# A list scheduler that keeps 64-column TensorE operations together, and attention weights made by a ScalarE Relu in the first three units

## The chip, the cores and the metric

The kernel runs on one core of a Trainium2 chip. The metric is device time in microseconds. The engines are named as the profile names them: PE is TensorE (PEld its weight loads), DVE is VectorE, ACT is ScalarE, POOL is GpSimd, SP is the queue that issues most transfers. Three timed runs of the kernel before are given, and one profiled execution.

## The reference

Input `x` has 64 graphs of 256 nodes with 256 features, and `adj` a 256 x 256 matrix of 0 and 1 for each graph. Four layers follow one another; each adds to `x` what it computes from `h = max(layernorm(x), 0)`.

- Layers 0 and 1 are graph attention with four heads of 64 columns. With `Wh = h W`, a score `e[i, j] = leaky_relu(src[i] + dst[j])` is masked by `adj`, goes through a softmax over `j`, and weighs `Wh`: `out[i] = sum_j softmax_j(e[i, j]) Wh[j]`. The slopes are 0.2 and 0.01. Layer 0 ends with an ELU; layer 1 adds a bias, a Relu, a residual and a layer norm over each head.
- Layer 2 is the same attention with one head of 256 columns (slope 0.2).
- Layer 3 is a gated graph network: three times, `m = h w[i]`, an aggregate over the neighbours `A^T m`, and a GRU cell with gates `r`, `z` and `n`.

## The kernel before, in words

The work is cut into 33 units: unit 0 is one graph, units 1 to 31 are two graphs each, unit 32 is the last graph. `graphs` (L976) describes a unit's four layers as operations. Nodes lie on the 128 partitions, so a unit of two graphs has four chunks of 128 nodes.

The softmax is taken apart. `factors` (L1077) makes, for each head, `cb`, the exponential of a node's score along a row, copied to all partitions, and `f`, two columns of exponentials for each partition. For the first two units `cb` comes from TensorE (`spread`, L1086); for the others it goes through DRAM (L1123, L1124). `weights` (L1139) builds the unnormalised weights `pt`: for each graph and half of its nodes a multiply by `f[1]` and a maximum with `f[0]` (L1145, VectorE, 256 columns), then for the whole head a minimum with `cap` (VectorE, 1024 columns). `cap` is made from the adjacency: it is huge where there is an edge and 0 or nearly 0 elsewhere, so the minimum is the mask. `attend_heads` (L1168) multiplies: for two heads, 32 matmuls whose weights are 128 x 64 pieces of `pt` and whose moving operand is `wh`, 65 columns, the last of which is 1 and gives the sum; two such matmuls with 64 columns each stand side by side in the array (L1163). `scaled` (L1180) then takes the reciprocal `rs` of the sum and writes `o`. Layer 2 uses the full 128 columns (L1163 too, 257 moving columns).

`gru` has, for each of three iterations and each half `j` of the features, four gates in PSUM banks from `ht` and `whh` and from the aggregate `ag` and `wc` (L1375, 512 moving columns; the bulk of TensorE's work). ScalarE applies tanh (L829, `g<-bank,bg` and `g<-g,bg`), VectorE combines them into the new `ht` half by half. Then each half of `ht` is transposed (L1389), split into two parts `hl` by a ScalarE copy and a VectorE subtraction, and aggregated (L1361); ScalarE copies the result to `ag`.

Every operation is recorded with an engine, a cost, what it reads and writes, and is put in order by `_Schedule.run` (L656). That is a list scheduler run when the program is built: it keeps a clock, a queue of operations that are ready for each engine, ordered by due time, and starts on an idle engine the first one whose buffers are free (L641). An operation is over after its cost, less an overlap of 90 on ScalarE and 80 on VectorE, and its result reaches another engine after a hop (OVERLAP and HOP, in ns). Operations marked `port` share one port between VectorE and POOL in this plan. What comes out is a fixed order of instructions on each engine, which the hardware then follows; the plan's times are not used again. So a changed cost can move operations far from the place where it was changed. Elementwise helpers record under one line, L829; the statistics are at L997 and L998, POOL's power at L1006, L1007, L1296 and L1297, the normalising Relu at L1015, `ht`'s first transposes at L1032, the projections at L1054, the masks at L1220 and L1230, the addition of layer 1 to `xt` at L1308.

Of the kernel before, what the change touches and what calls it, by code (L numbers as in the profile page):

```python
# [12 lines left out]
AF = mybir.ActivationFunctionType  # L13
# [503 lines left out]
SCORE_MAX = 40.0  # L517
SLOPES = (0.2, 0.01, 0.2)
SPREAD = 2
PACE = 104000.0  # L520


# [16 lines left out]
class _Op:  # L539
    __slots__ = (  # L540
        "engine", "cost", "port", "emit", "group", "bufs", "takes", "nbytes", "succs", "waits", "due", "ready",
        "index",
    )


class _Schedule:
# [28 lines left out]
    def buf(self, cls, shape, dtype=F32, tile=None):  # L575
        return _Buf(cls, shape, dtype, tile)

    def op(self, engine, cost, emit, reads=(), writes=(), takes=(), nbytes=0, port=False):
        o = _Op()
        o.port = port  # L580
        o.engine, o.cost, o.emit, o.group, o.nbytes = engine, cost, emit, self.group, nbytes
        o.succs, o.index, o.ready = [], len(self.ops), 0.0
        deps, o.bufs, o.takes = set(), [], []
        for written, items in ((False, reads), (True, writes)):
            for item in items:
                b, part = item if isinstance(item, tuple) else (item, None)
                if b not in o.bufs:
                    o.bufs.append(b)
                    b.left += 1
                if written and b.tile is None and b not in o.takes:  # L590
                    o.takes.append(b)
                keys = list(b.parts) if part is None else [k for k in (part, None) if k in b.parts]
                for k in keys:
                    writer, readers = b.parts[k]
                    if writer is not None:
                        deps.add(writer)
                    if written:
                        deps.update(readers)
                writer, readers = b.parts.get(part, (None, []))
                if written:  # L600
                    if part is None:
                        b.parts.clear()
                    b.parts[part] = (o.index, [])
                else:
                    b.parts[part] = (writer, readers + [o.index])
        for b in takes:
            if b.tile is None and b not in o.takes:
                o.takes.append(b)
        deps.discard(o.index)
        o.waits = len(deps)  # L610
        for d in deps:
            self.ops[d].succs.append(o)
        self.ops.append(o)
        return o
# [17 lines left out]
                )  # L632
            self.last[i.engine] = i.name

    def enable(self, ops, able):
        for o in ops:
            o.waits -= 1
            if o.waits == 0:
                heapq.heappush(able[o.engine], (o.due, o.index))

    def roomy(self, o):  # L641
        need = {}
# [13 lines left out]
    def run(self):  # L656
# [12 lines left out]
        events = []  # L669
        clock = self.dma_free = self.port_free = 0.0  # L670
        count = 0

        def post(t, kind, o):
            nonlocal count
# [8 lines left out]
        while True:  # L683
            for e in engines:
                if not idle[e]:
                    continue
                if e == "sp" and self.dma_free > clock + self.DMA_AHEAD:
                    continue
                held = []
                while able[e]:  # L690
                    item = heapq.heappop(able[e])
                    o = ops[item[1]]
                    if (not o.port or self.port_free <= clock) and self.roomy(o):
                        self.start(o, clock)
# [12 lines left out]
            while events and events[0][0] == clock:  # L707
                _, _, kind, o = heapq.heappop(events)
                if kind == "free":
                    idle[o.engine] = True  # L710
                    if o.nbytes:
                        self.dma_free = max(self.dma_free, clock) + o.nbytes / self.DMA_RATE
                        post(self.dma_free + self.DMA_LATENCY, "done", o)
                        post(max(clock, self.dma_free - self.DMA_AHEAD), "dma", o)
                    else:
                        post(clock + self.OVERLAP[o.engine] + self.HOP[o.engine], "done", o)
                    if o.engine == "pe":
                        self.enable([s for s in o.succs if s.engine == "pe"], able)
                elif kind == "done":
                    done += 1  # L720
                    self.enable([s for s in o.succs if s.engine != "pe" or o.engine != "pe"], able)
# [9 lines left out]
def _fast_path(  # L731
# [34 lines left out]
    nc = tc.nc  # L766
# [209 lines left out]
    def graphs(u, first, nb):  # L976
# [100 lines left out]
        def factors(wh, heads, width, slope, shift):  # L1077
# [55 lines left out]

            exps(0, 1.0)
            exps(1, slope)
            op("pool", 150, lambda: nc.gpsimd.memset(wh.tile[:, :, :, width], 1.0), [], [wh])  # L1136
            return f, cb

        def weights(cap, f, cb, h):  # L1139

            pt = buf("pt", [P, nb, 2, N])

            def emit(b, jc):
                c = 2 * b + jc
                nc.vector.tensor_scalar(  # L1145
                    pt.tile[:, b, jc, :].rearrange("p (i n) -> p i n", n=P),
                    cb.tile[:, h, 2 * b : 2 * b + 2, :],
                    f.tile[:, 1, h, c : c + 1], f.tile[:, 0, h, c : c + 1], op0=OP.mult, op1=OP.max,
                )

            for b in range(nb):
                for jc in range(2):
                    op("dve", 425, lambda b=b, jc=jc: emit(b, jc), [(cb, h), f], [(pt, (b, jc))], port=True)
# [14 lines left out]
        def attend_heads(o, o_view, pts, wh, hs):  # L1168
# [365 lines left out]
```

## Time and profile before

| what | value |
|---|---|
| median of three runs | 3197.43 us (3197.04 to 3197.9) |
| profiled execution, first to last instruction | 3198.1 us |
| mean granted TensorE clock in it | 0.996 |
| busy: PE, DVE, ACT, POOL | 3143.2, 2321.4, 1486.8, 897.4 us |
| matmuls of the gates, L1375, `wc` and `whh` | 1063.0 and 1055.6 us |
| matmuls with 64 weight columns, L1163, 128x65 | 263.7 us in 8192 records |
| multiply and maximum of the weights, L1145 | 416.9 us in 1152, 430 ns each |
| minimum with `cap`, 128x1024 | 326.1 us in 279, 1213 ns each |

The profile gives no time for its execution other than this span, which is 0.2 to 1.1 us longer than the timed runs. Matmuls of f32 leave two records each, transposes one. The duration of one instruction is longer than the distance between the starts of two neighbours, because they overlap; where many stand in a row the distance is what counts. A wait in brackets is idle time before the instruction, and what ended it.

### The profile page before, as it was taken

The page shows a single profiled execution, that of the slowest core. Times are in us where ns is not written, and L with a number is a line of the kernel's source. Part 1 is how long each engine was busy: PE and PEld are TensorE (multiplying, and loading weights), DVE is VectorE, ACT ScalarE, POOL GpSimd, SP SyncE. Part 2 cuts the span into 40 slices and gives each one's busy share as a digit, 9 for nine tenths or more (in the row PEclk, how much of TensorE's full clock was granted, in tenths as well). Part 3 has the DMA queues.
Part 4 walks back from the last instruction along what each step waited for, and adds up shares of the span by engine and source line. Part 5 has one row for each costly group of instructions (what it writes and reads, how often), then busy time and mean ns, then how long its engine had stood idle before and what let it go on. Part 6 is the DMA issues. An engine that isn't in the chain of part 4 may idle for free.

```text
span 3198.1 us, 48707 instructions
## 1 busy us (share of the span) xinstructions
PE 3143.2 (98%) x18599; PEld 1931.9 (60%) x18599; DVE 2321.4 (73%) x5206; ACT 1486.8 (46%) x3128; POOL 897.4 (28%) x907
## 2 busy tenths in 40 slices
PE   7899999999999999999999999999999999999998
PEld 6765656565666655566656566556566556665555
DVE  7777867778767778767678677788677787677753
ACT  5454444454454444454444454544444444544433
POOL 4323332133331233331233321333311333311210
PEclk9999999999999999999999999999999999999999
DMA  4110111101111101111101111111111011101000
GB/s 129 34 49 29 54 54 34 47 31 50 54 54 34 47 31 50 54 47 34 53 28 54 53 36 45 40 41 54 54 34 47 31 50 50 47 23 44 11 16 12
DMA packets 109927, 138.82 MB, mean 43 GB/s; under 512 B 44714, under 2 KB 97524, under 8 KB 102004
## 3 DMA queue, kind: packets, MB, share of 16 engines
q1 hardware_dynamic: 105712, 134.25, 12.8%
q8 instruction: 149, 2.44, 0.3%
q10 hardware_dynamic: 3972, 1.36, 0.2%
q14 instruction: 94, 0.77, 0.1%
HBM read 109.84 MB, written 17.34 MB: 40 GB/s over the span
## 4 chain that ended last, share of the span: by engine, by line
PE 87%; DVE 9%; POOL 2%; ACT 1%; issue 1%; DMA 0%; SPq 0%; ACTq 0%; POOLq 0%; DVEq 0%
PE bank L1375 55%; PE bank L1054 10%; PE bank L1163 10%; PE bank L1361 5%; PE bank L1032 3%; PE bank L1389 2%; DVE pt L1145 2%; DVE g L829 2%; DVE pt L829 1%; POOL mean L1297 1%; POOL o L829 1%; DVE o L829 1%; ACT ht L829 1%; DVE xt L1308 1%; DVE mean L829 1%
## 5 line engine op out<-in xcount | busy, mean ns | idle before, releaser
L1375 PE MATMUL bank<-ag,wc 128*128 128x512 f32 (+1 forms) x2376 | 1063.0, 582 | 0.0
L1375 PE MATMUL bank<-ht,whh 128*128 128x512 f32 (+1 forms) x2376 | 1055.6, 580 | 2.2 <-ACT g L829 1.3
L829 ACT ACTIVATE g<-bank,bg 128x512 f32<-128x512 f32 (+1 forms) x594 | 395.2, 670 | 713.6 <-PE bank L1375 706.6
L1375 PEld LDWEIGHTS bank<-ag,wc 128*128 128x128 f32 x2376 | 441.4, 190 | 459.2 <-issue 441.1
L1375 PEld LDWEIGHTS bank<-ht,whh 128*128 128x128 f32 x2376 | 435.0, 190 | 438.9 <-issue 424.2
L1006 POOL TENSOR_SCALAR mv<-mv 128x4 f32<-128x4 f32 (+1 forms) x132 | 81.9, 621 | 1428.6 <-DVE mv L998 1383.6
L1145 DVE TENSOR_SCALAR pt<-cb,f 128x256 f32<-128x256 f32 x1152 | 416.9, 430 | 6.0 <-ACT cb L1099 5.2
L1163 PEld LDWEIGHTS bank<-wh,pt 128*64 128x64 f32 (+1 forms) x8704 | 345.6, 142 | 94.4 <-issue 76.1
L829 DVE SCALAR_TENSOR_TENSOR g<-g,g 128x512 f32<-128x512 f32 (+1 forms) x396 | 263.3, 670 | 180.4 <-ACT g L829 180.4
L1163 PE MATMUL bank<-wh,pt 128*64 128x65 f32 (+1 forms) x8704 | 382.0, 233 | 9.7 <-DVE pt L829 5.8
L829 DVE TENSOR_TENSOR pt<-pt,cap 128x1024 f32<-128x1024 f32 (+1 forms) x297 | 341.3, 1193 | 0.1
L829 DVE SCALAR_TENSOR_TENSOR g<-bank,g 128x512 f32<-128x512 f32 (+1 forms) x198 | 129.8, 666 | 280.2 <-PE bank L1375 280.0
L829 DVE SCALAR_TENSOR_TENSOR g<-g,ht 128x512 f32<-128x512 f32 (+1 forms) x198 | 136.5, 689 | 172.0 <-ACT g L829 171.6
L1361 PE MATMUL bank<-am_r,hl 128*128 128x256 f32 x1536 | 238.1, 304 | 0.1
L1015 ACT ACTIVATE xn<-xt,mv 128x256 f32<-128x256 f32 x384 | 197.3, 588 | 72.1 <-DVE mv L829 71.9
L1361 PEld LDWEIGHTS bank<-am_r,hl 128*128 128x128 f32 x1536 | 198.2, 189 | 42.5 <-issue 30.6
L829 ACT COPY ag<-bank 128x512 f32<-128x512 f32 (+1 forms) x198 | 113.4, 573 | 233.4 <-PE bank L1361 230.1
L829 ACT ACTIVATE g<-g,bg 128x512 f32<-128x512 f32 (+1 forms) x198 | 137.6, 709 | 161.6 <-DVE g L829 159.4
L997 DVE BATCH_NORM_STATS2 st<-xt 128x6 f32<-128x256 f32 x512 | 208.1, 406 | 6.4 <-DMA xt<-in_x_dram 6.2
L829 ACT COPY ht<-bank 128x512 f32<-128x512 f32 (+1 forms) x264 | 137.8, 573 | 124.0 <-PE bank L1032 123.8
L1136 POOL MEMSET wh<- 128x16 f32 (+3 forms) x99 | 11.8, 120 | 635.5 <-ACT f L1130 635.5
L1007 POOL TENSOR_TENSOR mv<-mv,nhalf 128x4 f32<-128x4 f32 (+1 forms) x132 | 176.0, 1333 | 11.0
(91 smaller groups left out, 3452.2 us busy)
## 6 DMA issues: line engine op xcount, KB each, us to landing
cb<-rd SPq DMA_DIRECT2D x60, 1024.0 KB
xt<-in_x_dram SPq DMA_DIRECT2D x31, 512.0 KB
at<-in_adj_dram SPq DMA_DIRECT2D x31, 512.0 KB
out_dram<-xt SPq DMA_DIRECT2D x31, 512.0 KB
cb<-rd SPq DMA_DIRECT2D x30, 256.0 KB
cap<-cap_n SPq DMA_TRANSPOSE x128
cb<-rd SPq DMA_DIRECT2D x2, 512.0 KB
rd<-row ACTq DMA_DIRECT2D x60, 8.0 KB
```

Source lines behind the costliest of these rows:

```text
L829: emit = lambda: fn(*[a() if callable(a) else a for a in args], **kw)
L997: nc.vector.bn_stats(st.tile[:, c, :], xt.tile[:, c, :])
L1006: nc.gpsimd.tensor_scalar(mv.tile[:, 2, :], mv.tile[:, 1, :], 1e-5, None, op0=OP.add)
L1007: nc.gpsimd.tensor_tensor(mv.tile[:, 2, :], mv.tile[:, 2, :], nhalf[:, :C], op=OP.pow)
L1015: op("act", 610, lambda: nc.scalar.activation(xn.tile[:, c, :], xt.tile[:, c, :], AF.Relu, bias=mv.tile[:, 3, c : c + 1], scale=mv.tile[:, ...
L1032: nc.tensor.transpose(ps.tile[:, c * P : (c + 1) * P], xn.tile[:, c, dc * P : (dc + 1) * P], ident)
L1054: nc.tensor.matmul(ps.tile[:, : heads * W], lhsT=ht.tile[:, dc, c * P : (c + 1) * P], rhs=we[:, dc].rearrange("p h w -> p (h w)"), start=( ...
L1145: nc.vector.tensor_scalar(pt.tile[:, b, jc, :].rearrange("p (i n) -> p i n", n=P), cb.tile[:, h, 2 * b : 2 * b + 2, :], f.tile[:, 1, h, c ...
L1163: nc.tensor.matmul(ps[q * Q : (q + 1) * Q], lhsT=pt.tile[:, b, jc, i0 : i0 + Q], rhs=wh.tile[:, h, 2 * b + jc, :w], start=(jc == 0), stop= ...
L1361: nc.tensor.matmul(ps.tile[:, b * N : (b + 1) * N], lhsT=hl.tile[:, k, 2 * b + sc, :], rhs=am.tile[:, 2 * b + sc, :], start=(k == 0 and sc ...
L1375: nc.tensor.matmul(ps.tile[:, :S], lhsT=w[:, dc, g * P : (g + 1) * P], rhs=v.tile[:, dc, :], start=(first and dc == 0), stop=(last and dc ...
L1389: nc.tensor.transpose(ps.tile[:, c * P : (c + 1) * P], ht.tile[:, j, c * P : (c + 1) * P], ident)
```

## The change

It has three parts.

1. The scheduler knows a kind of TensorE operation, `tiled`, which only `attend_heads` sets. On TensorE it no longer takes the first ready operation with free buffers but asks `pick`: after a tiled operation it prefers another tiled one that is ready; otherwise it takes the first. `PATIENCE`, for which it would hold a lone tiled operation back, is 0. In the plan a tiled operation that follows another kind costs 250 ns more (`TILING`), and its own cost is 930 a head instead of 944 a head and 90.
2. In units 0, 1 and 2 (`LIFTED`) the weights are made in another way. ScalarE computes `relu(f[1] * cb - f[0])`, 256 columns at a time, and VectorE adds `f[0]` and takes the minimum with `cap` in one instruction, also 256 columns at a time. The sum is the same maximum as before. The minimum over the whole head is gone in these units.
3. For that, `f` has a third column, `-f[0]`, made by POOL in these units.

```diff
+LIFTED = 3
...
+    TILING = 250
+    PATIENCE = 0
...
-    def enable(self, ops, able):
+    def enable(self, ops, able, clock):
         for o in ops:
             o.waits -= 1
             if o.waits == 0:
+                o.ready = clock
                 heapq.heappush(able[o.engine], (o.due, o.index))
+
+    def pick(self, queue, clock, tiled):
+
+        first = None
+        for item in sorted(queue):
+            o = self.ops[item[1]]
+            if not self.roomy(o):
+                continue
+            if o.tiled and tiled:
+                first = item
+                break
+            if first is None:
+                first = item
+        if first is None:
+            return None
+        o = self.ops[first[1]]
+        if o.tiled and not tiled:
+            mates = sum(self.ops[i].tiled for _, i in queue)
+            if mates < 2 and clock - o.ready < self.PATIENCE:
...
+        queue.remove(first)
+        heapq.heapify(queue)
+        return first
...
+                if e == "pe":
+                    item = self.pick(able[e], clock, tiled)
+                    if item is not None:
+                        o = ops[item[1]]
+                        self.start(o, clock)
+                        idle[e] = False
+                        post(clock + o.cost + (self.TILING if o.tiled and not tiled else 0), "free", o)
+                        tiled = o.tiled
                     continue
...
-            f = buf("f", [P, 2, heads, C])
+            f = buf("f", [P, 3, heads, C])
...
+            if u < LIFTED:
+                op("pool", 150, lambda: nc.gpsimd.tensor_scalar(
+                    f.tile[:, 2], f.tile[:, 0], -1.0, None, op0=OP.mult), [(f, 0)], [(f, 2)])
...
+            def lifted(b, jc):
+                c = 2 * b + jc
+                view = lambda: pt.tile[:, b, jc, :]
+                op("act", 400, lambda: nc.scalar.activation(
+                    view().rearrange("p (i n) -> p i n", n=P), cb.tile[:, h, 2 * b : 2 * b + 2, :], AF.Relu,
+                    scale=f.tile[:, 1, h, c : c + 1], bias=f.tile[:, 2, h, c : c + 1],
+                ), [(cb, h), f], [(pt, (b, jc))])
+                vec(nc.vector.scalar_tensor_tensor, 425, view, view, lambda: f.tile[:, 0, h, c : c + 1],
+                    lambda: cap.tile[:, b, jc, :], op0=OP.add, op1=OP.min, reads=[f, cap],
+                    writes=[(pt, (b, jc))], port=True)
+
             for b in range(nb):
                 for jc in range(2):
+                    if u < LIFTED:
+                        lifted(b, jc)
+                        continue
                     op("dve", 425, lambda b=b, jc=jc: emit(b, jc), [(cb, h), f], [(pt, (b, jc))], port=True)
+            if u < LIFTED:
+                return pt
             vec(nc.vector.tensor_tensor, dve(1240), lambda: pt.tile, lambda: pt.tile, lambda: cap.tile, op=OP.min,
...
-            op("pe", pe(944) * len(hs) + 90, emit, [*pts, wh], banks_, takes=[o])
+            op("pe", pe(930) * len(hs), emit, [*pts, wh], banks_, takes=[o], tiled=True)
```

More of the change, by code (lines that the diff above doesn't have):

```diff
@@ L541 @@
         "engine", "cost", "port", "emit", "group", "bufs", "takes", "nbytes", "succs", "waits", "due", "ready",
-        "index",
+        "index", "tiled",
     )
@@ L576, in buf, with op @@
         return _Buf(cls, shape, dtype, tile)
-    def op(self, engine, cost, emit, reads=(), writes=(), takes=(), nbytes=0, port=False):
+    def op(self, engine, cost, emit, reads=(), writes=(), takes=(), nbytes=0, port=False, tiled=False):
         o = _Op()
+        o.tiled = tiled
         o.port = port
@@ L638, in enable @@
             if o.waits == 0:
+                o.ready = clock
                 heapq.heappush(able[o.engine], (o.due, o.index))
+    def pick(self, queue, clock, tiled):
[15 more added lines that the diff above has]
+            if mates < 2 and clock - o.ready < self.PATIENCE:
+                for item in sorted(queue):
+                    p = self.ops[item[1]]
+                    if not p.tiled and self.roomy(p):
+                        first = item
+                        break
+        queue.remove(first)
+        heapq.heapify(queue)
+        return first
     def roomy(self, o):
@@ L671, in run @@
         count = 0
+        tiled = False
         def post(t, kind, o):
@@ L717, in run @@
                     if o.engine == "pe":
-                        self.enable([s for s in o.succs if s.engine == "pe"], able)
+                        self.enable([s for s in o.succs if s.engine == "pe"], able, clock)
                 elif kind == "done":
                     done += 1
-                    self.enable([s for s in o.succs if s.engine != "pe" or o.engine != "pe"], able)
+                    self.enable([s for s in o.succs if s.engine != "pe" or o.engine != "pe"], able, clock)
                     for b in o.bufs:
@@ L1149, in emit @@
                 )
+            def lifted(b, jc):
[8 more added lines that the diff above has]
+                    writes=[(pt, (b, jc))], port=True)
             for b in range(nb):
                 for jc in range(2):
+                    if u < LIFTED:
+                        lifted(b, jc)
+                        continue
                     op("dve", 425, lambda b=b, jc=jc: emit(b, jc), [(cb, h), f], [(pt, (b, jc))], port=True)
+            if u < LIFTED:
+                return pt
             vec(nc.vector.tensor_tensor, dve(1240), lambda: pt.tile, lambda: pt.tile, lambda: cap.tile, op=OP.min,
```

## The prediction

> **What bounds the kernel now.** I read the page first (busy time, the chain that ended last), then busy time by stretches, then TensorE's timeline where a stretch is not full.
>
> ```profile
> PE 3143.2 (98%) x18599; PEld 1931.9 (60%) x18599; DVE 2321.4 (73%) x5206; ACT 1486.8 (46%) x3128; POOL 897.4 (28%) x907
> ...
> PE 87%; DVE 9%; POOL 2%; ACT 1%; issue 1%; DMA 0%; SPq 0%; ACTq 0%; POOLq 0%; DVEq 0%
> ```
>
> TensorE works 98% of the span and is 87% of the chain. So a gain can come only from TensorE work that goes away or from TensorE waits that go away: 3198.1 - 3143.2 = 54.9 us of waits, and the slow clock after them. The stretches say where they are (columns: stretch, length, busy time of PE, PEld, DVE, ACT, POOL with instruction counts, granted clock, DMA).
>
> ```profile
> 80.00:90.00 10.00, 4.15 (x125) 4.04 (x121) 9.07 (x25) 0.00 (x0) 1.57 (x3) 0.79 0.01 2
> 90.00:100.00 10.00, 6.89 (x121) 6.04 (x119) 9.79 (x30) 3.30 (x7) 3.70 (x4) 0.84 0.01 2
> 100.00:120.00 20.00, 15.01 (x58) 11.04 (x56) 15.98 (x40) 11.21 (x29) 15.34 (x18) 0.84 0.16 41
> ...
> 1000.00:2000.00 1000.00, 998.25 (x5885) 604.82 (x5883) 741.13 (x1644) 468.69 (x977) 283.54 (x273) 1.00 0.14 45
> ```
>
> Up to 120 us TensorE is starved, VectorE is full from 80 to 100 and ScalarE nearly empty; after that TensorE is full. In the first 120 us its timeline shows this (start, length, what, wait in brackets):
>
> ```profile
> 88.78 3.74 PE L1163 MATMUL bank<-wh,pt 128*64 128x65 f32 x64 [5.85 <-DVE pt L829]
> ...
> 109.74 1.04 PE L1032 MATMUL bank<-ident,xn 128*128 128x128 f32 x8
> ...
> 115.08 0.33 PE L1032 MATMUL bank<-ident,hn 128*128 128x128 f32 x1
> ```
>
> The 5.85 us are a wait for VectorE's attention weights; the 64 records after it last 3.74 us, where the same 64 last 2.08 elsewhere: the clock fell too. In the full stretch one small thing repeats in every unit:
>
> ```profile
> 1608.82 2.08 PE L1163 MATMUL bank<-wh,pt 128*64 128x65 f32 x64
> 1610.84 1.98 PE L1375 MATMUL bank<-ag,wc 128*128 128x512 f32 x4
> 1612.75 2.08 PE L1163 MATMUL bank<-wh,pt 128*64 128x65 f32 x64
> ...
> 1629.77 1.04 PE L1389 MATMUL bank<-ident,ht 128*128 128x128 f32 x8
> 1630.64 1.88 PE L1375 MATMUL bank<-ht,whh 128*128 128x512 f32 x4
> ...
> 1647.90 3.96 PE L1163 MATMUL bank<-wh,pt 128*64 128x65 f32 x128
> 1651.79 1.10 PE L1032 MATMUL bank<-ident,xn 128*128 128x128 f32 x8
> 1652.73 0.65 PE L1389 MATMUL bank<-ident,ht 128*128 128x128 f32 x4
> 1653.56 0.63 PE L1389 MATMUL bank<-ident,ht 128*128 128x128 f32 x4 [0.17 <-ACT ht L829]
> 1654.03 1.88 PE L1375 MATMUL bank<-ht,whh 128*128 128x512 f32 x4
> ```
>
> Eight transposes of `ht` take 0.87 us from start to start where nothing waits (1629.77 to 1630.64), but 1.30 us here (1652.73 to 1654.03): 0.17 us of visible wait and 0.26 us of restart, 0.43 us together. The waits of this line between 300 and 3000 us are 26 in number, once a unit. What VectorE does just before:
>
> ```profile
> 1648.92 0.68 DVE L1308 TENSOR_TENSOR xt<-xt,o 128x512 f32<-128x512 f32 x1
> ...
> 1650.13 0.41 DVE L997 BATCH_NORM_STATS2 st<-xt 128x6 f32<-128x256 f32 x1
> ...
> 1652.76 0.66 DVE L829 SCALAR_TENSOR_TENSOR ht<-g,g 128x512 f32<-128x512 f32 x1
> ```
>
> The second `ht` (the second half of the line at 1652.76, ending at 1653.42) is what the transposes at 1653.56 need. Before it VectorE ran L1308's `xt` addition (0.61 us) and one statistics pair (0.55 us), which nobody needs yet.
>
> **What the Trainium skill says.** "TensorEngine Tiling (Array Packing)", section Tiling Modes, says that changing the tiling mode drains TensorE. The trace agrees: a lone operation of 64-column tiles, with the gate after it, takes 1608.82 to 1612.75 = 3.93 us, of which the gate is 1.72, so 2.21 alone; two in a row take 1647.90 to 1651.79 = 3.89 and some 0.15 around it, 4.04. One joining is worth 0.3 to 0.4 us. "TensorE: Matmul & The Clock Gate", Part 1, says that about 3.4 us of idling halves the clock; the 3.74 against 2.08 agrees. "ScalarE: Activation LUTs", section What ACT_TABLE_LOAD costs, gives an activation 186 ns + 0.833 ns a column, 93 ns more for each per-partition operand, and 93 ns of overlap between neighbours: 585 ns for the new Relu. The trace has the same form, L1015's Relu, at 588 ns alone and 2.07 us for four in a row, 0.495 us each. The planner counts the new one at 400 - 90 = 0.31.
>
> **The change, part by part.**
>
> *The grouping.* I counted the built order of TensorE's instructions. The 64-column operations stand in 99 stretches before and in 101 after (three more in the first units, one fewer at the end, where two meet). In the repeating unit they stand as before: one, one gate, one, and later two together; `PATIENCE` is 0, so nothing is ever held back for a mate. So the named effect is not there: +2 x 0.3 = +0.6 us.
>
> *What the new costs do to the order of a repeating unit.* On TensorE only the aggregate (L1361) moves back by one gate. On VectorE the `xt` addition and the statistics pair now stand behind both `ht`, and ScalarE takes the last `z` before the two `n`. I follow the new order with the durations above: last `z` read at 1648.15 after the last gate's end at 1647.97, ready 1648.84; second `d` by 1649.6; the two `n` by 1650.1; both products by 1650.85; first `ht` by 1651.6; then VectorE waits for the second tiled operation's banks (TensorE ends it at 1651.86, some 0.2 us to get through), two reciprocals, second `ht` by 1652.9. TensorE comes to the second block at 1651.79 + 0.94 + 0.44 = 1653.17. The wait is gone with 0.15 us to spare: -0.43 x 26 = -11.2 us. What is late next: the recurrent gate's input `wc` now has one gate instead of two to hide ScalarE's copy of the aggregate. The aggregate would end at 1658.94, the copy at 1659.75, the gate comes at 1660.66: 0.9 us in hand. In the last iteration the second `ht` now stands behind an `o` product that waits for POOL's power, and comes at about 1629.3 against a need at 1630.06: 0.75 us in hand. Cost 0 for both; without that cover, see the rivals.
>
> *The lifted weights in units 0 to 2.* Per pair of images and head VectorE did four multiply-max at 0.325 us (5.25 us for 16 in a row) and one minimum at 1.155 (4.62 for four); it now does four add-minimum. That form with a bf16 operand is not in the trace; the f32 two-input form on 256 columns has 0.42 alone, 0.33 in a row, and 0.47 beside a busy POOL: I take 0.33, so 1.32 instead of 2.46. A single image saves 0.6 (1.26 to 0.66). Up to unit 0's GRU the order has 12 of the first and 9 of the second: 12 x 1.14 + 9 x 0.6 = -19 us of VectorE (-13 with 0.47). ScalarE gets 12 x 4 + 9 x 2 = 66 Relus x 0.495 = +32.7 us (+20 if the planner's 0.31 were true). ScalarE had 56 us up to 110 us (the ten stretches' sum, 51, and half the next); with 33 more it is busy 89 us from its first activation at 9.2: about 98 us without a gap. So VectorE stops being the bound there and ScalarE takes its place. Behind the Relus on ScalarE's queue stand copies that TensorE waits for: unit 0's second projection is copied only after 16 Relus (I find about 1.3 us of wait), the third unit's between Relus (some 2 us in all), and while unit 1's second layer runs each attend waits for its own Relus. Following this the second layer-2 attend of unit 0 ends at about 98 to 100, where before it ended at 109.7. But part is given back. Before, between that attend and the transposes of `hn` TensorE had 0.87 + 3.56 = 4.4 us of other work to do while `hn` was made (109.74 to 115.08); in the new order these stand elsewhere and `hn` comes next, so TensorE waits for the whole chain. -10 + 4.5 = -5.5 us. Ends: -11 (the chain is hidden after all) and +4 (Relus stall TensorE in unit 0's GRU, where 24 more of them come and a gate is only 0.86 us).
>
> *The rest.* Nine negations on POOL (the nearest row, a small scalar operation, is 0.24 us) stand in front of the first Relu of each layer; POOL is 28% busy, but in the first 35 us it is near the path: 0 to +0.5 us, inside the range above. SP's queue has the same loads, some in another place (adjacency before transposes); before, hardly any wait of TensorE fell on a load after 15 us: 0. The Relu's table was loaded already for L1015. The end of the program has the same TensorE order: 0.
>
> Sum: -11.2 - 5.5 + 0.6 = -16 us. Against the profiled span 3198.1 that is 3182; the runs' median, 3197.4, is 0.7 below that span, which gives 3181.5.
>
> **Rivals.** (1) The repeating wait stays: the second `ht` has only 0.15 us to spare, and a later `z` or a slower hop through the reciprocals would keep it. Then only the start gains: 3197.4 - 5.5 + 0.6 = 3192.5. For it: the narrow margin. Against: 1.1 us of VectorE work has left the path. (2) ScalarE's Relus eat the start's gain: it decides when they and their waits cost 10 us more than I count, so that the attend ends at 109 again. Then 3197.4 - 11.2 + 0.6, about 3187, or a few us more. For it: the planner's 0.31 against 0.495. Against: ScalarE idles 13.28 us in one piece there now. (3) Slower: the `o` product placed before the last iteration's second `ht` holds VectorE until POOL's power is ready. If POOL comes more than 0.75 us later than before, TensorE waits in all 28 units; at 0.85 us of wait each, +24, which gives 3205. It turns slower from about 0.6 us a unit on. For it: POOL's order changed in the same unit. Against: the same POOL work stands before that power. (4) The grouping does save switches: 30 joinings would be -10 us; the count of the built order speaks against it, and I give it no chance of its own.
>
> **How the numbers follow.** My forecast has 0.55, the repeating wait that stays 0.18, ScalarE eating the start 0.17, slower 0.10. What a measurement here can tell from no change is about 0.2%, 6.4 us. Faster than that (under 3191): nearly all of the first, most of the third and a little of the second, 0.70; same 0.19; slower 0.11. The forecast's own range is 3174 to 3190 (start between -11 and +2, margin of the repeating wait). To leave out no more than 2 in 10 the range takes in the waits that stay: 3173 to 3197.
>
> **What would show it.** Right: no wait on the `ht` transposes between 300 and 3000 us, eight of them 0.87 us apart in every unit; ScalarE full and VectorE with gaps from 70 to 100 us; unit 0's layer-2 attends near 97 and a wait of some 5 us before the `hn` transposes. Wrong: a wait of about 0.4 us or more in each unit at any TensorE line, a Relu of 0.4 us, or the attend later than 106.

## The result, and the profile after

The changed kernel takes 3222.28 us (median of five runs, 3221.98 to 3223.07), the kernel before 3197.43 beside it: a ratio of 1.0077, 95% interval 1.0064 to 1.0089. It is slower by 25 us, outside the range; 3181.5 was forecast. The profiled span is 3220.5 us against 3198.1.

The page of the changed kernel, busy time and the chain that ended last:

```profile
PE 3147.7 (98%) x18599; PEld 1931.9 (60%) x18599; DVE 2340.3 (73%) x5179; ACT 1517.4 (47%) x3218; POOL 934.4 (29%) x916
...
PE 69%; DVE 16%; POOL 10%; ACT 2%; issue 2%; DMA 0%; POOLq 0%; ACTq 0%; SPq 0%; DVEq 0%
```

TensorE has the same work (3147.7 us busy against 3143.2) and 72.8 us without any, against 54.9. In the chain, VectorE and POOL have gone from 11% to 26%: something on those two now stands between TensorE's instructions, over most of the span. The stretches (length, then busy time of PE, PEld, DVE, ACT, POOL with counts, granted clock, DMA) say where:

```profile
80.00:90.00 10.00, 8.46 (x150) 7.21 (x149) 7.62 (x20) 10.00 (x24) 0.00 (x0) 1.00 0.01 2
90.00:100.00 10.00, 5.45 (x135) 4.79 (x134) 9.50 (x21) 5.87 (x15) 2.90 (x4) 0.96 0.01 2
100.00:120.00 20.00, 13.01 (x44) 9.98 (x44) 17.27 (x43) 9.93 (x26) 15.75 (x16) 0.68 0.16 40
1000.00:2000.00 1000.00, 990.73 (x5800) 599.88 (x5799) 738.59 (x1605) 465.47 (x980) 294.59 (x272) 1.00 0.13 44
```

From 1000 to 2000 us TensorE is busy 990.73 us where it had 998.25: that is 7.5 us lost in one thousand, in the part that repeats. From 80 to 90 us it does gain, and ScalarE is full there, as forecast; from 100 to 120 it has 13.01 us at a clock of 0.68, against 15.01 at 0.84.

TensorE's timeline in one repeating unit (start, length, what, wait in brackets; 15.12 us after the same piece of work in the kernel before):

```profile
1644.88 0.60 PE L1450 MATMUL bank<-ident,ht 128*128 128x128 f32 x4
1646.40 0.63 PE L1450 MATMUL bank<-ident,ht 128*128 128x128 f32 x4 [0.92 <-DVE ht L871]
1646.86 1.88 PE L1436 MATMUL bank<-ht,whh 128*128 128x512 f32 x4
...
1668.01 1.09 PE L1074 MATMUL bank<-ident,xn 128*128 128x128 f32 x8
1668.94 1.15 PE L1450 MATMUL bank<-ident,ht 128*128 128x128 f32 x8
1669.93 3.61 PE L1436 MATMUL bank<-ht,whh 128*128 128x512 f32 x8
```

Two blocks of `ht` transposes were followed in the prediction. The second one here, behind the two 64-column operations, needed 1.30 us before; now it goes from 1668.94 to 1669.93, 0.99 us, and its wait is gone. The first one took 0.87 us before; it is now cut in two, and from its start to the gate behind it are 1.98 us, 1.11 more, of which 0.92 is the visible wait for `ht`. The waits of the whole stretch from 300 to 3000 us show it in nearly every unit, 23.0 us in 24 places, where the kernel before had 5.2 us of waits for `ht` in 26:

```profile
PE bank L1450 <- DVE ht L871: 23.0, 24, 1.3
```

What VectorE and POOL do before it, in the changed kernel:

```profile
1630.80 1.57 DVE L871 SCALAR_TENSOR_TENSOR g<-g,g 128x512 f32<-128x512 f32 x1
1632.29 0.74 DVE L871 TENSOR_TENSOR o<-bank,rs 128x256 f32<-128x256 f32 x2
...
1644.96 0.69 DVE L871 TENSOR_TENSOR o<-o,mean 128x512 f32<-128x512 f32 x1 [1.54 <-POOL mean L1358]
1645.57 0.68 DVE L871 SCALAR_TENSOR_TENSOR ht<-g,g 128x512 f32<-128x512 f32 x1
```

```profile
1630.55 1.27 POOL L871 TENSOR_TENSOR hl<-hn,hl 128x512 fp32r<-128x512 f32 x1 [0.27 <-ACT hl L1407]
1633.11 1.27 POOL L871 TENSOR_TENSOR o<-o,bias_b 128x512 f32<-128x512 f32 x1 [1.29 <-DVE o L871]
...
1642.97 1.96 POOL L1358 TENSOR_TENSOR mean<-mean,nhalf 128x8 f32<-128x8 f32 x1
```

And the same instructions in the kernel before, VectorE's first, then POOL's:

```profile
1615.72 0.72 DVE L829 TENSOR_TENSOR o<-bank,rs 128x256 f32<-128x256 f32 x2
...
1617.90 0.68 DVE L829 SCALAR_TENSOR_TENSOR g<-g,g 128x512 f32<-128x512 f32 x1
```

```profile
1616.69 1.28 POOL L829 TENSOR_TENSOR o<-o,bias_b 128x512 f32<-128x512 f32 x1
...
1626.29 1.97 POOL L1297 TENSOR_TENSOR mean<-mean,nhalf 128x8 f32<-128x8 f32 x1
```

VectorE stands 1.54 us at the product `o<-o,mean`, waiting for POOL's power, and `ht` is behind it. That is the place and the mechanism of rival (3). The power ends at 1642.97 + 1.96 = 1644.93; less the 15.12 us between the two kernels that is 1629.81, and in the kernel before it ended at 1626.29 + 1.97 = 1628.26. It is 1.55 us late. The first lines of the views show where this begins: `g<-g,g` stood behind the two `o` before and stands in front of them now; it takes 1.57 us instead of 0.68, beside POOL's subtraction `hl`; the two `o` are therefore late; and POOL's bias addition waits 1.29 us for them, where before it had no wait. The other units agree: between 300 and 3000 us the bias additions wait 78.9 us for `o` (45.0 before), and the products `o<-o,mean` 57.7 us for POOL's power (0.3 before).

To add up by place I use one quantity, TensorE's delay: the start of a piece of its work in the trace, less the full-rate time of all TensorE work ahead of it. Only differences between kernels at the same amount of work are used, so the rates drop out. A difference can move by 1 to 2 us with the place at which it is read, since the orders differ.

| TensorE work ahead | before, delay | after, against before |
|---|---|---|
| 80 us | 49.3 us | +1.2 |
| 300 us | 52.5 us | +4.2 |
| 2900 us | 92.3 us | +27.1 |
| end | 106.5 us | +23.6 |

So the start loses 4 us (forecast: gains 5.5), the repeating units lose 23 (forecast: gain 11.2), and the last ones win 3.5 (forecast: nothing). From one repeating unit to the next TensorE takes 97.8 us, where it took 96.9: 1.1 us are lost at the first block of `ht` transposes and 0.3 won at the second. In the 23 units that have this wait that makes some 20 of the 23 us.

### The profile page after: what moved, and what is told of

Read it like the earlier page. It is cut to its first block, busy times and chain, and to the rows that moved or that the text cites. A ratio compares the mean times of both kernels' runs of the same rounds, so it can differ in the third digit from the quotient of the medians.

```text
span 3220.5 us, 48992 instructions
## 1 busy us (share of the span) xinstructions
PE 3147.7 (98%) x18599; PEld 1931.9 (60%) x18599; DVE 2340.3 (73%) x5179; ACT 1517.4 (47%) x3218; POOL 934.4 (29%) x916
## 4 chain that ended last, share of the span: by engine, by line
PE 69%; DVE 16%; POOL 10%; ACT 2%; issue 2%; DMA 0%; POOLq 0%; ACTq 0%; SPq 0%; DVEq 0%
PE bank L1436 43%; PE bank L1096 10%; PE bank L1224 7%; DVE pt L1190 5%; PE bank L1422 3%; POOL cap_n L1291 3%; PE bank L1074 3%; PE bank L1450 2%; DVE g L871 2%; DVE pt L871 2%; DVE o L871 2%; POOL mv L1049 2%; DVE st L1039 1%; POOL mean L1358 1%; POOL mv L1048 1%
## 5 line engine op out<-in xcount | busy, mean ns | idle before, releaser
L871 DVE SCALAR_TENSOR_TENSOR g<-g,g 128x512 f32<-128x512 f32 (+1 forms) x396 | 282.3, 723 | 199.4 <-ACT g L871 199.4
L1190 DVE TENSOR_SCALAR pt<-cb,f 128x256 f32<-128x256 f32 x1062 | 387.7, 432 | 1.8 <-DMA cb<-rd 1.6
L871 DVE TENSOR_TENSOR pt<-pt,cap 128x1024 f32<-128x1024 f32 (+1 forms) x270 | 311.7, 1196 | 0.0
L1049 POOL TENSOR_TENSOR mv<-mv,nhalf 128x4 f32<-128x4 f32 (+1 forms) x132 | 184.2, 1396 | 11.0
```

The costliest lines, as they stand in the source:

```text
L871: emit = lambda: fn(*[a() if callable(a) else a for a in args], **kw)
L1049: nc.gpsimd.tensor_tensor(mv.tile[:, 2, :], mv.tile[:, 2, :], nhalf[:, :C], op=OP.pow)
L1190: nc.vector.tensor_scalar(pt.tile[:, b, jc, :].rearrange("p (i n) -> p i n", n=P), cb.tile[:, h, 2 * b : 2 * b + 2, :], f.tile[:, 1, h, c ...
```

## Which part of the change does it

Times below are medians; the kernel before had 3198.1 to 3198.5 in the same series. "Delay" is against the kernel before, at the places of the table.

**The lifted weights taken out (e1).**

```diff
-LIFTED = 3
+LIFTED = 0
```

> The changed kernel with LIFTED = 0: all attention weights by VectorE again as before, the grouping and its costs kept. The built order of a repeating unit is the same as in the changed kernel, instruction by instruction, on all five engines. My theory (the 1.09 us wait at the second block of ht transposes, once a unit, makes the change slower, and the start adds 2 to 3): about 3219, the wait of 0.9 us still there in every unit. Rival (the lifted weights make it slower, by ScalarE or by what they leave behind): back to about 3197.

Measured 3220.3 us, ratio 1.0068 (1.0051 to 1.0085). The loss stays, all but 2 us, so the lifted weights are not what makes it. Delay +1.1 at 300 us of work, +25.7 at 2900.

**Only the preference kept (e2).**

```diff
-LIFTED = 3
+LIFTED = 0
-    TILING = 250
+    TILING = 0
-            op("pe", pe(930) * len(hs), emit, [*pts, wh], banks_, takes=[o], tiled=True)
+            op("pe", pe(944) * len(hs) + 90, emit, [*pts, wh], banks_, takes=[o], tiled=True)
```

> The changed kernel with LIFTED = 0 and with the planner's old cost of a 64-column operation (944 a head and 90, no 250 for a switch): only the preference for a second such operation is left. The built order of a repeating unit is that of the kernel before on all engines. My theory (the costs move the order, not the preference): 3197, within 3. Rival (the preference itself costs time, by holding other work back): 3205 or more.

Measured 3200.2 us, ratio 1.0003 (0.9995 to 1.0012): no difference that can be told from none. The preference, which gives the change its name, neither makes the loss nor brings a gain.

**Only the planner's costs (e9), and one of them alone (e5).** e9 is the changed kernel with

```diff
-LIFTED = 3
+LIFTED = 0
-            if o.tiled and tiled:
+            if False:
```

and e5 the kernel before with one number changed:

```diff
-            op("pe", pe(944) * len(hs) + 90, emit, [*pts, wh], banks_, takes=[o])
+            op("pe", pe(930) * len(hs), emit, [*pts, wh], banks_, takes=[o])
```

> The changed kernel with LIFTED = 0 and without the preference: only the planner's costs of a 64-column operation are new (930 a head, and 250 when it follows another kind). The built order of a repeating unit is that of the changed kernel on all five engines. My theory (the costs alone bring that order, and the order brings the wait): 3219 to 3222, with TensorE's wait for ht 23 us between 300 and 3000 us. Rival (the preference is needed): 3197 to 3205.

> The kernel before with one number changed: the planner counts a pair of 64-column heads at 1860 ns instead of 1978; no preference, no charge for a switch, no lifted weights. The built order of a repeating unit is then that of the changed kernel on all five engines. My theory (the order of the repeating unit makes the change slower, and this cost is what moves it): 3218 to 3222. Rival (the preference or the lifted weights are needed for it): 3197 to 3203.

e9 measured 3218.7 us, ratio 1.0067 (1.0050 to 1.0084), with 24.8 us of waits for `ht`: the costs alone bring the order and the loss. e5 measured 3215.6 us, ratio 1.0053 (1.0036 to 1.0070), but its expectation rests on a false premise. Its built order is neither that of the kernel before nor that of the changed one; it is a third, with other waits. The longest group of TensorE's waits in e5 from 300 to 3000 us:

```profile
PE bank L1032 <- DVE g L829: 9.1, 15, 1.9
```

So e5 says nothing on the wait at `ht`. It shows something else: 118 ns less on one planned cost gave an order with waits of its own, and it was 17 us slower.

## What makes ht late

**The product moved behind ht (e3).** The planner's order is kept. When a VectorE instruction marked `prod` is due, its emission is held until the next VectorE instruction, if that is marked `ht`:

```diff
+    BEHIND, ONCE = {"prod": ("ht",)}, "ht"
...
+        if o.kind in self.BEHIND and self.holds(o):
+            self.kept = o
+        else:
+            self.issue(o)
+            if self.kept is not None and o.kind == self.ONCE:
+                self.release()
...
+                sched.kind = "prod"
                 vec(nc.vector.tensor_mul, dve(700), og, og, lambda: wide(var), reads=[var], writes=part, port=True)
...
+                    sched.kind = "ht"
                     vec(stt, dve(700), lambda: h_new.tile[:, j, :], lambda: d.tile, 2 * half, lambda: n.tile,
```

> The changed kernel with one VectorE instruction moved: where the product with POOL's power stands directly before an ht, it goes directly behind it, 27 places in the program, 25 of them one a unit. All other engines keep their order. My theory (this product holds VectorE for POOL and the ht behind it is what TensorE waits for): the wait of 0.9 us at the second block of transposes goes, -0.92 to -1.09 in 25 units, 3195 to 3199 in all, with the product's later end (0.6 us) hidden behind POOL's second power. Rival (the wait moves on to POOL's gamma and beta and the xt addition behind them): 3215 to 3222. Rival (POOL or ScalarE make ht late): no change.

Measured 3216.0 us, ratio 1.0055 (1.0039 to 1.0072). My theory fell, and the first rival named the number. TensorE's timeline of e3 in the same unit:

```profile
1643.08 1.04 PE L1477 MATMUL bank<-ident,ht 128*128 128x128 f32 x8
1643.96 1.88 PE L1463 MATMUL bank<-ht,whh 128*128 128x512 f32 x4
...
1665.10 1.09 PE L1100 MATMUL bank<-ident,xn 128*128 128x128 f32 x8
1666.47 1.40 PE L1477 MATMUL bank<-ident,ht 128*128 128x128 f32 x8 [0.28 <-DVE ht L897]
1667.71 2.75 PE L1463 MATMUL bank<-ht,whh 128*128 128x512 f32 x6
```

The first block has no wait any more. But the second block, 23 us later, waits again: from 1665.10 to the gate at 1667.71 are 2.61 us, where 0.94 for `xn` and 0.87 for `ht` would do, 0.80 lost. VectorE's timeline of e3 in between:

```profile
1645.55 1.75 DVE L897 TENSOR_TENSOR o<-o,mean 128x512 f32<-128x512 f32 x1 [1.14 <-POOL mean L1384]
...
1648.46 1.74 DVE L1396 TENSOR_TENSOR xt<-xt,o 128x512 f32<-128x512 f32 x1 [0.56 <-POOL o L897]
1650.13 6.20 DVE L1216 TENSOR_SCALAR pt<-cb,f 128x256 f32<-128x256 f32 x16
...
1666.51 0.66 DVE L897 SCALAR_TENSOR_TENSOR ht<-g,g 128x512 f32<-128x512 f32 x1
```

Follow it: the second product waits 1.14 us for POOL's second power, the `xt` addition (L1396) waits for POOL's `o` behind it, and from there to `ht` at 1666.51 VectorE has no gap: 6.20 us of attention weights, 4.62 of minima, then the gate's chain. I measure from the start of the first block of transposes. The `xt` addition comes 3.83 us after it in the kernel before (1633.60 less 1629.77) and 5.38 us after it here; TensorE needs the second `ht` 23.4 us after it in both, and here it is done at 24.09. POOL's lateness has gone past the first `ht` and reached the second. In the changed kernel the 1.1 us lost at the first block had hidden it, since they gave VectorE time.

**The slow product moved (e4).** The same means; `g<-g,g` goes behind the two `o` products:

```diff
+    BEHIND, ONCE = {"rn": ("sc",)}, None
+    def holds(self, o):
+        return self.before_dve == "rs"
...
+                sched.kind = "sc"
                 vec(nc.vector.tensor_mul, dve(420), lambda: o_view(h), lambda: view()[:, :, :E],
...
+                    sched.kind = "rn"
                     vec(stt, dve(700), lambda: n.tile, lambda: r.tile, 1.0, lambda: n.tile,
```

> The changed kernel with another VectorE instruction moved, once a unit: the product g of r and n, which runs 1.57 us beside POOL's subtraction, goes behind the two o products that it stood before. My theory (this slow product makes o late, o makes POOL's bias addition wait 1.29 us, and so the power comes late): POOL's bias addition starts some 1.3 us earlier, the product waits 0.2 to 0.4 us for the power instead of 1.54, TensorE's wait of 0.9 us goes to 0.1 or nothing: 3196 to 3201. Rival (the power is late by POOL's own order, cap_n four in a row and hl): TensorE's wait stays above 0.6 us, 3214 to 3222.

Measured 3205.8 us, ratio 1.0021 (1.0014 to 1.0029): 16.5 us of the loss are back by one VectorE instruction standing two places further on. VectorE and POOL of e4, the same piece of work:

```profile
1624.07 0.85 DVE L897 SCALAR_TENSOR_TENSOR g<-g,g 128x512 f32<-128x512 f32 x1
...
1636.68 0.69 DVE L897 TENSOR_TENSOR o<-o,mean 128x512 f32<-128x512 f32 x1 [1.54 <-POOL mean L1386]
```

```profile
1623.10 1.28 POOL L897 TENSOR_TENSOR hl<-hn,hl 128x512 fp32r<-128x512 f32 x1 [0.26 <-ACT hl L1435]
1624.33 1.72 POOL L897 TENSOR_TENSOR o<-o,bias_b 128x512 f32<-128x512 f32 x1
```

`g<-g,g` takes 0.85 us instead of 1.57, and POOL's bias addition comes without a wait, 1.33 us earlier against TensorE's work (it starts 13.10 us before the first block of transposes, 11.77 in the changed kernel). So the lateness begins where I read it. The expectation missed in size, by 5 us. VectorE itself also comes earlier, and so the product still waits 1.54 us; and POOL's addition now meets `g<-g,g` and takes 1.72 us instead of 1.27. The first block takes 1.15 us (1637.43 to 1638.58) instead of 0.87: 0.28 us a unit stay, some 7 us in all.

**Both moves, without the lifted weights (e6), and with them (e11).** e11 is the changed kernel with this and with the marks of both; e6 has `LIFTED = 0` as well.

```diff
+    BEHIND, ONCE = {"prod": ("ht",), "rn": ("sc",)}, "ht"
+    def holds(self, o):
+        return o.kind == "prod" or self.before_dve == "rs"
```

> The changed kernel with LIFTED = 0 and with both moves of the last two experiments: the product g of r and n behind the two o products, and the product with POOL's power behind the ht. My theory (POOL's late power is the source; with it early, VectorE is early too, and the product behind ht takes the last 0.26 us of wait away): no wait over 0.1 us at either block of ht transposes, some 0.28 us a unit less than the kernel before, 3190 to 3196. Rival (VectorE is then late at the block after the two 64-column operations, as it was when the product alone was moved): 3203 or more.

> The whole change (LIFTED = 3 too) with both moves of one VectorE instruction. My theory: the two moves give back the 25 to 30 us that they gave without the lifted weights, and the start keeps its loss of 1 to 3: 3192 to 3194. Rival (the lifted start leaves the later units late): over 3198.

e6 measured 3190.9 us, ratio 0.9977 (0.9968 to 0.9985): as expected, and faster than both kernels. Of the waits for `ht` from 300 to 3000 us, 23.0 us in the changed kernel, e6 has one left:

```profile
PE bank L1479 <- DVE ht L897: 1.3, 1, 1.3
```

and both blocks run through:

```profile
1626.63 1.04 PE L1479 MATMUL bank<-ident,ht 128*128 128x128 f32 x8
1627.50 1.88 PE L1465 MATMUL bank<-ht,whh 128*128 128x512 f32 x4
...
1649.58 1.11 PE L1479 MATMUL bank<-ident,ht 128*128 128x128 f32 x8
1650.52 3.60 PE L1465 MATMUL bank<-ht,whh 128*128 128x512 f32 x8
```

0.87 us for the first and 0.94 for the second. So the order that the new costs gave was not a bad one: with two VectorE instructions moved, its repeating units take less than those of the kernel before (delay between 300 and 2900 us of work: 35.3 us against 39.8). e11 measured 3196.8 us, ratio 0.9995 (0.9987 to 1.0004), above the 3192 to 3194 that I expected: the lifted weights cost 5.9 us here, nearly all of it before 500 us of work (delay +0.1 there for e6, +5.7 for e11).

**The grouping for once made true (e7).**

```diff
-LIFTED = 3
+LIFTED = 0
-    PATIENCE = 0
+    PATIENCE = 2000
```

> The changed kernel with LIFTED = 0 and PATIENCE = 2000: a 64-column operation is held back up to 2 us for a second one. The built order now has 66 stretches of them instead of 101: both pairs of a unit stand together. If a joining is worth the 0.3 us that I read before, and nothing else waits: -33 x 0.3 = -10 us against the kernel before, 3188. Rival (the new order of the unit has waits of its own on ht, wc or o, as in the changed kernel, which has nothing to do with the joining): 3200 to 3225.

Measured 3218.9 us, ratio 1.0063 (1.0046 to 1.0080). The joinings are there, 66 stretches for 101, and their gain of some 10 us, if it is there too, is more than paid for by other waits. The longest group of TensorE's waits in e7 from 300 to 3000 us:

```profile
PE bank L1096 <- DVE o L871: 7.8, 9, 0.9
```

It falls on a line, the projections, that hardly waited before. What a joining is worth remains the estimate from the trace of before; no run isolates it.

## What the lifted weights do

**The lifted weights alone (e10).** `LIFTED` stays 3; the planner's costs are the old ones.

```diff
-    TILING = 250
+    TILING = 0
-            op("pe", pe(930) * len(hs), emit, [*pts, wh], banks_, takes=[o], tiled=True)
+            op("pe", pe(944) * len(hs) + 90, emit, [*pts, wh], banks_, takes=[o])
```

Without its mark `tiled` the preference is off too, where the expectation has it on; by e2 it makes no difference.

> The changed kernel with the planner's old costs: the lifted weights of units 0 to 2 and the preference, and the built order of a repeating unit is that of the kernel before on all five engines. My theory (the lifted weights lose about 3 us in the start and nothing else): 3200 to 3203. Rival (they gain in the start what I predicted, and only the other order hid it): 3192 to 3195.

Measured 3210.2 us, ratio 1.0037 (1.0023 to 1.0051): slower than both theories had it. Delay +10.7 at 300 us of work, and +12.1 at 2900: nearly everything is lost in the start. So in all three pairs that differ by the lifted weights these cost time, but how much depends on the order around them: some 2 us (the changed kernel less e1), 5.9 (e11 less e6), and 12.0 here. Its waits differ from those of the changed kernel's start, for the costs set that order too; but the largest is in the same place. TensorE of the changed kernel, then of e10:

```profile
99.65 3.48 PE L1224 MATMUL bank<-wh,pt 128*128 128x257 f32 x8 [3.53 <-DVE pt L871]
110.00 1.40 PE L1074 MATMUL bank<-ident,hn 128*128 128x128 f32 x4 [6.86 <-ACT hn L1057]
```

```profile
115.29 1.39 PE L1074 MATMUL bank<-ident,hn 128*128 128x128 f32 x4 [8.60 <-ACT hn L1057]
```

The changed kernel ends unit 0's layer-2 attends at 99.65 + 3.48 = 103.1, where 98 to 100 was forecast, and is then 6.5 us ahead of the kernel before (delay 38.9 against 45.4 us). Then TensorE stands 6.86 us for `hn`. The chain behind it is longer too, 6.9 us from the end of the attends to `hn` where the kernel before had 5.2: POOL has its two powers of 1.67 and 1.64 us from 102.07 on, ahead of the one that `hn` needs (105.82), and VectorE's small `mv` product behind that takes 1.22 us at 108.09. Then the clock. The stretch from 110 to 120 us of the changed kernel, and then those from 100 to 120 us of the kernel before:

```profile
110.00:120.00 10.00, 9.87 (x36) 8.04 (x37) 7.54 (x20) 6.35 (x20) 7.95 (x9) 0.69 0.15 53
```

```profile
100.00:110.00 10.00, 6.31 (x19) 4.68 (x18) 8.04 (x19) 4.39 (x11) 6.54 (x9) 0.69 0.07 14
110.00:120.00 10.00, 8.71 (x42) 6.35 (x39) 7.94 (x22) 6.82 (x18) 8.80 (x10) 1.00 0.24 67
```

TensorE is full there (9.87 us) at a clock of 0.69, where before it had 1.00: some 3 us of its work are lost (busy time times the missing part of the clock). Before, the same slow clock fell into the stretch from 100 to 110 us, with 6.31 us of work in ten, and cost some 2 us by the same reckoning. So I estimate the clock's part in the difference at 1 to 2 us. What the earlier attends had won is gone at 80 us of work (+1.2), and smaller waits, of which 0.9 us for ScalarE's `row` at 272 us is the longest, make it +4.2.

**The price of the add-and-minimum (e8, e12).** I had taken 0.33 us in a row. In the changed kernel eight in a row take 3.93 us, 0.49 each. e8 puts an f32 operand in the place of the bf16 one, e12 a constant in the place of the per-partition operand.

```diff
 e8
-                    lambda: cap.tile[:, b, jc, :], op0=OP.add, op1=OP.min, reads=[f, cap],
+                    view, op0=OP.add, op1=OP.max, reads=[f, cap],
 e12
-                vec(nc.vector.scalar_tensor_tensor, 425, view, view, lambda: f.tile[:, 0, h, c : c + 1],
+                vec(nc.vector.scalar_tensor_tensor, 425, view, view, 1.0,
```

> The changed kernel with the bf16 cap of the lifted weights' add-and-minimum replaced by the f32 tile itself, with a maximum: the mask is left out, the order of all engines is the same. It tells what made this instruction 0.49 us in a row where I took 0.33. If the bf16 operand costs the time: 0.33 in a row. If two inputs from SBUF do, or ScalarE's and POOL's traffic beside it: 0.49 still. Time within 4 us of the changed kernel's either way.

> The changed kernel with the add-and-minimum's per-partition operand replaced by the constant 1.0: the attention weights are then wrong by a factor for each row, the order of all engines is the same. It tells what made this instruction 0.49 us in a row, since the f32 operand did not shorten it. If the operand read from SBUF costs it: 0.33 in a row. If not, 0.49, and then it is two inputs of 256 columns beside ScalarE's writes, or something that I have not named. Time within 4 us of the changed kernel's.

One run each: 3222.3 and 3224.2 us. This instruction's durations in the first 300 us (count; least, median, longest in ns), in the changed kernel, e8 and e12:

```profile
L871 DVE SCALAR_TENSOR_TENSOR pt<-pt,f,cap x90: 451/484/1418, 22.2 to 242.8; 128x256 f32<-128x256 f32 x90
```

```profile
L871 DVE SCALAR_TENSOR_TENSOR pt<-pt,f x90: 452/484/1418, 22.9 to 242.6; 128x256 f32<-128x256 f32 x90
```

```profile
L871 DVE SCALAR_TENSOR_TENSOR pt<-pt,cap x90: 393/425/1361, 22.9 to 244.8; 128x256 f32<-128x256 f32 x90
```

The operand's type makes no difference (484 ns for both); the per-partition operand costs 59 ns (425). Where they follow the Relus neither matters: 15 of them take 7.35 us in the changed kernel and in e8, and 7.29 in e12, and ScalarE's Relus come 0.50 us apart (eight in 4.07 us). At one place all ten Relus were done before the first of ten add-and-minimums began. ScalarE and VectorE of the changed kernel there, then VectorE of e8 and of e12:

```profile
150.04 5.02 ACT L1199 ACTIVATE pt<-cb,f 128x256 f32<-128x256 f32 x10
```

```profile
155.61 4.01 DVE L871 SCALAR_TENSOR_TENSOR pt<-pt,f,cap 128x256 f32<-128x256 f32 x10
```

```profile
155.41 4.02 DVE L871 SCALAR_TENSOR_TENSOR pt<-pt,f 128x256 f32<-128x256 f32 x10
```

```profile
157.65 3.41 DVE L871 SCALAR_TENSOR_TENSOR pt<-pt,cap 128x256 f32<-128x256 f32 x10
```

With nothing to wait for they take 0.40 us each, and 0.34 without the per-partition operand. So the 0.49 in a row is ScalarE's pace, which VectorE follows; VectorE's own price is 0.40, and of what this exceeds the 0.33 that I took nearly all is the per-partition operand.

## Why the prediction was wrong, step by step

*The grouping, +0.6: not contradicted.* The changed kernel has the 101 stretches that were counted, and the preference alone makes no difference (e2). A price of 0.6 us is too small for these runs to show.

*The repeating wait of 0.43 us goes, -11.2: held for the most part, by itself.* The second block takes 0.99 us instead of 1.30; of the 0.15 us to spare nothing is left, and 0.12 us of the wait remain. That is 0.31 us a unit instead of 0.43, some 7 to 8 us.

*"0.75 us in hand" at the last iteration's second `ht`, costed at nothing: this step failed.* I had seen that `ht` stands behind a product that waits for POOL, and took POOL's power to be as early as before because the same POOL work stands ahead of it. The work was the same; what that work waits for was not. `g<-g,g`, which the prediction doesn't name, had moved in front of the `o` products and beside POOL's subtraction; it took 1.57 us where it took 0.68 before, and POOL's chain came 1.55 us late (e4 shows the link, e3 and e6 that the product and `ht` carry it to TensorE). The cover was too large as well: in the trace `ht` ends 1.32 us after the power (1646.25 less 1644.93), so that with a power at 1628.26 it is ready at 1629.58, not at 1629.3, and 0.48 us are in hand against the need at 1630.06. 1.55 less 0.48 is the 1.1 us that TensorE lost. Rival (3) had the mechanism and 0.85 us of wait a unit, turning slower from 0.6; the trace has 1.1, and 23 us in all between 300 and 2900 us of work. Its chance of 0.10 was too small for a cover of less than 1 us that three engines had to keep.

*The start, -5.5: wrong in sign, by 9.7 in all, and no single term does it.* The attends came 6.5 us earlier, where I had 10. The wait for `hn` took back about 6 instead of 4.5. A term that I left out, the slow clock after this long wait, and what else lies before 80 us of work bring another 1.7. The smaller waits between 80 and 300 us of work add 3.0; I had none. Relus at 0.50 us in a row were right (0.495); the add-and-minimum was sized at 0.33 and came at 0.49, since it follows the Relus.

*The end, 0: wrong by 3.5 in the change's favour.* A wait of 1.3 us for ScalarE's `g` in the last units is gone. Another 1.6 us are the clock: behind the same wait for `ht`, 1.85 us in both, the same eight records of gate matmuls take 3.44 us in the kernel before and 1.89 in the changed one,

```profile
3174.66 3.44 PE L1375 MATMUL bank<-ht,whh 128*128 128x256 f32 x8
```

```profile
3199.99 1.89 PE L1436 MATMUL bank<-ht,whh 128*128 128x256 f32 x8
```

at a granted clock of 0.61 (3174 to 3178 us) and of 1.00 (3199 to 3203). Behind a wait of the same length e7 and e10 show the slow clock at this place too (2.92 and 3.29 us), e1 and e2 don't (1.89). Whether the change decides it or the luck of one execution is not shown.

## What to carry to other kernels

When a change alters the costs of a planner, the order of every engine is new, and each instruction that stands in another place has to be priced by who now runs beside it, above all VectorE instructions next to POOL's. A cover of less than a microsecond that rests on another engine being as early as before is not a cover until that engine's own inputs have been followed. A wait that is taken away at one place can come back at the next, as in e3, if its source is a chain on two other engines: look for the instruction where the lateness begins, as e4 did, and move that.

## What the runs showed of the hardware

A VectorE instruction can stand still for as long as a POOL instruction runs, and the profile counts that time as its own duration, not as a wait. In the lines above `g<-g,g` starts at 1630.80, POOL's subtraction, which began before it, ends at 1631.82, and `g<-g,g` ends 0.55 us later, at 1632.37. In e4 it starts at 1624.07, POOL's subtraction ends at 1624.38, and it ends 0.54 us after that. Whether 1.02 or 0.31 us of POOL's instruction were left, the end comes the same time behind it, as if `g<-g,g` did its work only then. In e4 the other side shows too: POOL's bias addition begins while `g<-g,g` runs and takes 1.72 us instead of 1.27. The Trainium skill says so in "SBUF — State Buffer", section SBUF: two separate sides: a VectorE instruction with two SBUF inputs and a GpSimd instruction that reads SBUF share a pair of ports, whichever starts first has it for the whole instruction, and the other is blocked. The trace agrees. The cost here was 0.9 us on VectorE in each unit, which reached TensorE by way of POOL. e4, which takes these 0.9 us and the instruction's own 0.6 out from in front of the two `o`, gave back 16.5 of the 25 us; no run separates the two shares.
